# A graph network's first LayerNorm scaled on ScalarE, with a power, a leaky step and a maximum placed anew and the weights' preparation spread over the first iterations

## The chip, the cores and the metric

The kernel runs on one core of a Trainium2 chip. The metric is the device time of one execution in microseconds (us). Engines: PE is TensorE's matmuls, PEld its weight loads, DVE is VectorE, ACT is ScalarE, POOL is GpSimd. SBUF and PSUM are the two memories that the kernel's tiles are declared in; its matmuls write tiles of PSUM, in what the kernel calls banks. The granted clock is the share of TensorE's full clock that the profile's clock records show: 1.00 is full. The profiles are single executions; the times are medians.

## The reference, cut to what matters

Two layers over 128 graphs of 128 nodes with 512 features.

```python
# layer 0: graph attention (8 heads of 64), residual, LayerNorm "a"
feats = einsum('bnf,hfu->bhnu', X, W)
dense = leaky_relu(e_self[..., :, None] + e_neigh[..., None, :], 0.2)
dense = dense + NEG_BIG * (1.0 - A)
x = layernorm(x + relu(softmax(dense) @ feats + b))
# layer 1: two hypergraph convolutions, the first with relu and a LayerNorm behind it; residual; LayerNorm "o"
h = layer_norm(relu(hypergraph_conv(x, adj, W1, b1)), gamma, beta)
x = layernorm(x + hypergraph_conv(h, adj, W2, b2) + x)
```

## The kernel before

64 pairs of graphs go through a software pipeline. Iteration t runs stage 0 of pair t, stage 1 of pair t-1, and so on to stage 4. Each step has a lag and a time within the iteration (a period is some 43 us), and the steps' order by that time is the order of every engine's instructions.

The parts that matter: the mask is added on POOL, the leaky step is on ACT, the maximum on DVE.

```python
    for (g, q), tm, (lag, tl), (lagx, tx), te in (
        ((0, 0), 33.0, (1, 34.9), (1, 37.3), 9.5), ((0, 1), 34.3, (1, 36.2), (1, 38.3), 10.8),
        ((1, 0), 35.6, (1, 40.6), (2, 3.5), 12.6), ((1, 1), 36.9, (2, 2.9), (2, 4.3), 13.9),
    ):
        at(1, tm, masked, g, q)          # POOL, 128x512
        at(lag, tl, leaky, g, q)         # ACT, four of 128x128
        at(lagx, tx, largest, g, q)      # DVE
```

The first LayerNorm ("a"): statistics on DVE, the power on POOL as the end of the second graph's statistics, the scaling on DVE.

```python
    def moments(p, s, key, t, g):
        ... # bn_stats, bn_aggr
        if g == 1:  # the lines that allocate the tiles are cut
            nc.vector.tensor_scalar(ve, s["mv", key][:, :, 1], EPS, None, op0=ALU.add)
            nc.gpsimd.tensor_tensor(s["rs", key], ve, mhalf, op=ALU.pow)

    def normalize(s, key, t, g):
        nc.vector.tensor_scalar(t, t, s["mv", key][:, g, 0:1], s["rs", key][:, g:g + 1],
                                op0=ALU.subtract, op1=ALU.mult)

    at(2, 31.3, residual, 0)
    at(2, 33.2, residual, 1)
    @step(2, 35.7)
    def first_output(p, s):
        for g in range(2):
            normalize(s, "a", s["y"][:, g, :], g)
```

The matrix products are done as seven smaller ones in a chain. Products 1, 6, 7 and 4 use the PSUM bank X; ACT copies it out three times on the way. In the chain `py`, product 4 (time 39.2) must wait, by the program, until the third copy (time 38.0) has read the bank.

```python
    chain("py", 3, (29.2, 30.95, 32.7, 34.4, 36.2, 39.2, 40.9, 31.0, 34.5, 38.0), weigh,
          QU, 1)
    # seven products in the order 1, 2, 6, 5, 7, 4, 3, then ACT's three copies of bank X
```

The preparation of the weights stands in blocks: `prepare_first()` ahead of the loop, `prepare_hidden()` and `prepare_output()` at the end of iteration 1, `prepare_output_blocks()` (16 scalings and four block sums of 128x1024, all on DVE) ahead of iteration 2. `nodes` (time 10.4, DVE) makes the two scaled adjacency matrices of a pair.

## Time and profile before

| | before |
|---|---|
| time, median of 3 (range) | 2877.6 us (2877.2 to 2879.2) |
| profiled execution, span | 2872.6 us |
| mean granted TensorE clock | 0.990 |
| PE's waits for ACT's third copy of py | 69.3 us, 62 times |
| first pz matmul (layer 1 of the first pair) | 106.76 us |

Two of these numbers divide the run: up to the first pz matmul the pipeline fills, and PE idles a good part of the time; from there on PE is the bound, and its only recurring idle time is the wait for that copy. The lines themselves are in the prediction.

### The profile page before, as it was taken

To read this page: it belongs to the slowest core of one execution; us is meant where nothing else is said; L and a number is where in the kernel's file an instruction comes from. 1 tells how busy PE (TensorE), PEld (TensorE's weight loads), DVE (VectorE), ACT (ScalarE), POOL (GpSimd) and SP (SyncE) were. 2 spreads that over 40 slices of the span, in tenths; PEclk is the share of its full clock that TensorE was granted. 3 is DMA by queue.
4 is the path that set the end of the run, shared out by engine and by line. 5 is a ranking of instruction groups with operands and counts; after the bars stand their busy time and mean duration, and the time that the engine had idled before them with its cause. 6 is when DMAs were issued, how large, how long until landed. Compare 5 with 4: busy or idle time off the path is not lost.

```text
span 2872.6 us, 50435 instructions
## 1 busy us (share of the span) xinstructions
PE 2718.0 (95%) x18272; PEld 2476.4 (86%) x18272; DVE 1904.6 (66%) x4335; ACT 1590.2 (55%) x4549; POOL 1714.7 (60%) x1806
## 2 busy tenths in 40 slices
PE   3799999999999999999999999999999999999997
PEld 2688888888988888988988988988988988988986
DVE  4566666676676676676676676676676676676664
ACT  1465565565565555555555655655655655655652
POOL 3356656656656656656656656656656566566554
PEclk8799999999999999999999999999999999999999
DMA  4111111112112112112112112111112112112110
GB/s 143 45 48 61 60 47 62 59 44 65 58 44 67 46 55 67 46 56 67 45 56 67 42 60 67 43 59 67 42 60 67 42 60 67 42 60 67 41 38 23
DMA packets 99660, 161.61 MB, mean 56 GB/s; under 512 B 11602, under 2 KB 48466, under 8 KB 99412
## 3 DMA queue, kind: packets, MB, share of 16 engines
q1 hardware_dynamic: 95424, 156.80, 17.2%
q8 instruction: 146, 2.39, 0.3%
q10 hardware_dynamic: 3988, 1.59, 0.3%
q14 instruction: 102, 0.84, 0.1%
HBM read 124.27 MB, written 34.08 MB: 55 GB/s over the span
## 4 chain that ended last, share of the span: by engine, by line
PE 61%; POOL 21%; DVE 9%; ACT 6%; issue 3%; DMA 1%; POOLq 0%; SPq 0%; DVEq 0%; ACTq 0%
PE phX L615 16%; POOL hS L369 8%; PE phW L615 8%; PE pyX L387 8%; POOL sq L666 8%; PE pyW L387 5%; DVE y L533 5%; PE pz L579 4%; PE phY L615 4%; PE pfX L387 4%; PE pq L736 4%; DVE statsa L541 2%; PE pav L502 2%; ACT nb L449 2%; POOL nb L442 2%
## 5 line engine op out<-in xcount | busy, mean ns | idle before, releaser
L449 ACT ACTIVATE nb<-nb,ft 128x128 f32<-128x128 f32 x1024 | 327.0, 391 | 171.1 <-POOL nb L442 161.0
L442 POOL TENSOR_TENSOR nb<-nb,neg 128x512 f32<-128x512 f32 x256 | 343.1, 1361 | 101.1 <-DMA nb<-rd 101.1
L615 PEld LDWEIGHTS phX<-zS,w_sb 128*128 128x128 f32 x3072 | 363.0, 192 | 31.3 <-issue 31.3
L615 PE MATMUL phX<-zS,w_sb 128*128 128x128 f32 x3072 | 374.2, 275 | 0.8 <-ACT ph L254 0.8
L254 ACT COPY py<-pyX 128x257 f32<-128x257 f32 (+1 forms) x192 | 70.4, 366 | 490.7 <-PE pyX L387 490.7
L666 POOL TENSOR_TENSOR sq<-sq 128x512 f32<-128x512 f32 (+2 forms) x384 | 311.1, 817 | 20.1
L387 PE MATMUL pyX<-w_sb,h 128*128 128x257 f32 (+1 forms) x1024 | 253.1, 389 | 69.5 <-ACT py L254 69.3
L462 ACT ACTIVATE nb<-nb,nm 128x128 f32<-128x128 f32 x1024 | 312.9, 391 | 0.0
L645 ACT ACTIVATE h<-h,b_sb 128x128 f32<-128x128 f32 x768 | 244.5, 390 | 116.1 <-DVE h L630 116.1
L547 POOL TENSOR_TENSOR rso<-veo,mhalf 128x2 f32<-128x2 f32 x64 | 44.9, 701 | 421.0 <-DVE veo L545 421.0
L369 POOL TENSOR_TENSOR hS<-h 128x512 f32<-128x512 f32 x128 | 160.1, 1272 | 180.0 <-ACT h L645 180.0
L387 PEld LDWEIGHTS pyX<-w_sb,h 128*128 128x128 f32 x1024 | 184.2, 190 | 95.9 <-ACT py L254 74.9
L387 PE MATMUL pyX<-w_sb,hS 128*128 128x257 f32 (+1 forms) x1024 | 244.3, 381 | 2.5 <-POOL hS L369 2.5
L533 DVE SCALAR_TENSOR_TENSOR y<-y,x 128x512 f32<-128x512 f32 x128 | 184.5, 1441 | 91.6 <-POOL y L526 91.6
L387 PE MATMUL pyW<-w_sb,hS 128*128 128x256 f32 x1024 | 242.4, 378 | 2.1 <-DVE y L698 2.1
L502 PE MATMUL pav<-ft,eT 128*128 128x65 f32 x2048 | 239.5, 272 | 1.9 <-ACT eT L489 1.9
L502 PEld LDWEIGHTS pav<-ft,eT 128*128 128x128 f32 x2048 | 237.4, 192 | 2.1 <-ACT eT L489 2.1
L387 PEld LDWEIGHTS pyX<-w_sb,hS 128*128 128x128 f32 x1024 | 194.7, 190 | 31.5 <-POOL hS L369 2.9
L387 PEld LDWEIGHTS pyW<-w_sb,hS 128*128 128x128 f32 x1024 | 193.6, 189 | 30.4 <-DVE y L698 2.5
L550 DVE TENSOR_SCALAR y<-y,mva,rsa 128x512 f32<-128x512 f32 x128 | 183.2, 1470 | 52.2 <-POOL rsa L547 52.2
L603 POOL TENSOR_TENSOR zS<-zT 128x256 f32<-128x256 f32 x128 | 93.4, 730 | 205.3 <-ACT zT L590 205.3
L410 DVE TENSOR_TENSOR ft<-pf,pfW 128x264 f32<-128x264 f32 x128 | 55.1, 430 | 237.9 <-ACT pf L254 167.5
(128 smaller groups left out, 6167.9 us busy)
## 6 DMA issues: line engine op xcount, KB each, us to landing
nb<-rd SPq DMA_DIRECT2D x128, 512.0 KB, 4.5
x<-in_x_dram SPq DMA_DIRECT2D x64, 512.0 KB, 5.9
out_dram<-o SPq DMA_DIRECT2D x64, 512.0 KB, 2.8
a<-in_adj_dram SPq DMA_DIRECT2D x64, 128.0 KB, 5.0
w<-in_adj_dram SPq DMA_DIRECT2D x128, 64.0 KB, 4.8
w_sb<-in_w1t_dram SPq DMA_DIRECT2D x3, 512.0 KB, 6.5
w_sb<-in_w2t_dram SPq DMA_DIRECT2D x3, 512.0 KB, 9.6
w_raw<-in_w_dram SPq DMA_DIRECT2D x4, 256.0 KB, 4.7
```

The source lines that it names most:

```text
L369: engine.tensor_tensor(t[:, i], in0, in1, op=op)
L387: nc.tensor.matmul(to[:, :n], lhs[:, k, :], rhs[:, k, :n], start=bool(start) and k == 0, stop=(k == nk - 1), skip_group_check=True,)
L442: nc.gpsimd.tensor_tensor(t, t, s["neg"][:, g, None, :].to_broadcast([P, HH, N]), op=ALU.add)
L449: nc.scalar.activation(t, t, AF.Prelu, bias=s["ft"][:, g, h, 0:1], alpha=SLOPE)
L462: nc.scalar.activation(t, t, AF.Exp, bias=s["nm"][:, g, h:h + 1])
L502: nc.tensor.matmul(t[:, h * (U + 1):(h + 1) * (U + 1)], s["eT"][:, g, q * HH + h, :], s["ft"][:, g, q * HH + h, 2:], start=True, stop=True,)
L533: nc.vector.scalar_tensor_tensor(y, y, 0.0, s["x"][:, g, :], op0=ALU.max, op1=ALU.add)
L550: nc.vector.tensor_scalar(t, t, s["mv", key][:, g, 0:1], s["rs", key][:, g:g + 1], op0=ALU.subtract, op1=ALU.mult,)
L579: nc.tensor.matmul(t[:, k * N:(k + 1) * N], s["y"][:, g, k * P:(k + 1) * P], s["R"][:, g, :], start=True, stop=True,)
L615: nc.tensor.matmul(to[:, m * N:(m + 1) * N], w[:, k, m * P:(m + 1) * P], rhs[:, k, :], start=bool(start) and m == 0 and k == 0, stop=(k == ...
L645: nc.scalar.activation(dst[:, k, :], src[:, k, :], AF.Relu, bias=b1_sb[:, c:c + 1])
L666: nc.gpsimd.tensor_tensor(t[:, :n, :], t[:, :n, :], t[:, n:2 * n, :], op=ALU.add)
```

## The change

Its intent has two parts. In the steady state, the leaky step of the second mask leaves ACT's queue ahead of the third copy of `py`, so that PE's wait gets shorter; the scaling of LayerNorm "a" moves from DVE to ACT, as `Identity(rs * y + sh)` with a small new DVE instruction for `sh = -mean * rs`. At the start, the weights' preparation is cut into pieces among the first iterations, so that PE gets work earlier.

```diff
-    ... ((0, 1), 34.3, (1, 36.2), (1, 38.3), 10.8),
+    ... ((0, 1), 34.3, (1, 39.8), (1, 40.9), 10.8),
         # the power leaves moments() and becomes a step behind the second mask (34.3)
+    at(2, 35.5, rstds, "a")
-    @step(2, 35.7)
-    def first_output(p, s):
-        for g in range(2):
-            normalize(s, "a", s["y"][:, g, :], g)
+    @step(2, 36.3)
+    def first_shift(p, s):
+        s["sh"] = small.tile([P, 2], F32, tag="sh", name=f"sh_{p}")
+        nc.vector.scalar_tensor_tensor(
+            s["sh"], s["mv", "a"][:, :, 0], -1.0, s["rs", "a"], op0=ALU.mult, op1=ALU.mult)
+    def first_output(p, s, g):
+        t = s["y"][:, g, :]
+        nc.scalar.activation(
+            t, t, AF.Identity, bias=s["sh"][:, g:g + 1], scale=s["rs", "a"][:, g:g + 1])
+    at(2, 36.6, first_output, 0)
+    at(2, 37.2, first_output, 1)
-    at(3, 38.5, y_sum, 1, 1, 2, "W")
+    at(3, 38.4, y_sum, 1, 1, 2, "W")
+    at(4, 15.7, rstds, "o")
         # preparation: load of the first x later; block sums and memsets on POOL instead of DVE
-        second_sums(nc.vector, [w2_sb[:, i, :, :QU] for i in range(7)], w2_12)
+        second_sums(nc.gpsimd, [w2_sb[:, i, :, :QU] for i in range(7)], w2_12)
+    once = {
+        0: [(11.0, prepare_first)],
+        1: [(27.7, prepare_hidden), (27.5, prepare_output), (28.0, prepare_output_sums)],
+        2: [(9.0, prepare_output_blocks), (9.5, prepare_output_block_sums)],
+    }
+        # in iteration 2, stage 1's steps before time 30 stand 17 earlier
```

More of the change, by code (lines that the diff above doesn't have):

```diff
@@ L94, in load, with load_x @@
             nc.sync.dma_start(s["w"][:, g, :], adj[2 * p + g, 0, :].partition_broadcast(P))
+        if p:
+            load_x(p)
+    def load_x(p):
+        s = st[p]
         s["x"] = work.tile([P, 2, F], F32, tag="x", name=f"x_{p}", bufs=3)
-        nc.sync.dma_start(s["x"], x[gs].rearrange("g n f -> n g f"))
+        nc.sync.dma_start(s["x"], x[2 * p:2 * p + 2].rearrange("g n f -> n g f"))
     load(0)
@@ L124 @@
     an_bc = spread(a_neigh, F, "an_bc")
+    load_x(0)
     b0_bc = spread(b0, F, "b0_bc")
@@ L187, in prepare_hidden @@
         nc.vector.tensor_tensor(s4, a12, s2, op=ALU.subtract)
+    gbs = const.tile([P, KH, 2], F32, name="gbs")
+    made = {}
     def prepare_output():
-        gbs = const.tile([P, KH, 2], F32, name="gbs")
         nc.vector.tensor_scalar(gbs[:, :, 0], gb[:, 0, :], 1.0 / DH, None, op0=ALU.mult)
         nc.vector.tensor_copy(gbs[:, :, 1], gb[:, 1, :])
-        pv = [bank(f"pv{j}") for j in range(2)]
+        pv = made["pv"] = [bank(f"pv{j}") for j in range(2)]
         for blk, i, j in w2_blocks:
@@ L201, in prepare_output, with prepare_output_sums @@
                 )
+    def prepare_output_sums():
+        pv = made["pv"]
         sums = const.tile([2, F], F32, name="sums")
@@ L209, in prepare_output, with prepare_output_blocks @@
             nc.scalar.dma_start(t, sums_d[c].partition_broadcast(P))
-        return gw
-    def prepare_output_blocks(gw):
+        made["gw"] = gw
+    def prepare_output_blocks():
+        gw = made["gw"]
         for blk, i, j in w2_blocks:
@@ L219, in prepare_output_blocks, with prepare_output_block_sums @@
                 )
-        second_sums(nc.vector, [w2_sb[:, i, :, :QU] for i in range(7)], w2_12)
+    def prepare_output_block_sums():
+        second_sums(nc.gpsimd, [w2_sb[:, i, :, :QU] for i in range(7)], w2_12)
         for i in (0, 1, 5):
-            nc.vector.memset(w2_sb[:, i, :, QU:], 1.0 / DH)
+            nc.gpsimd.memset(w2_sb[:, i, :, QU:], 1.0 / DH)
     steps = []
@@ L464 @@
     for (g, q), tm, (lag, tl), (lagx, tx), te in (
-        ((0, 0), 33.0, (1, 34.9), (1, 37.3), 9.5), ((0, 1), 34.3, (1, 36.2), (1, 38.3), 10.8),
+        ((0, 0), 33.0, (1, 34.9), (1, 37.3), 9.5), ((0, 1), 34.3, (1, 39.8), (1, 40.9), 10.8),
         ((1, 0), 35.6, (1, 40.6), (2, 3.5), 12.6), ((1, 1), 36.9, (2, 2.9), (2, 4.3), 13.9),
@@ L542, in moments, with rstds @@
         nc.vector.bn_aggr(s["mv", key][:, g, :], stats)
-        if g == 1:
-            ve = small.tile([P, 2], F32, tag="ve", name=f"ve{key}_{p}")
-            nc.vector.tensor_scalar(ve, s["mv", key][:, :, 1], EPS, None, op0=ALU.add)
-            s["rs", key] = small.tile([P, 2], F32, tag="rs", name=f"rs{key}_{p}")
-            nc.gpsimd.tensor_tensor(s["rs", key], ve, mhalf, op=ALU.pow)
+    def rstds(p, s, key):
+        ve = small.tile([P, 2], F32, tag="ve", name=f"ve{key}_{p}")
+        nc.vector.tensor_scalar(ve, s["mv", key][:, :, 1], EPS, None, op0=ALU.add)
+        s["rs", key] = small.tile([P, 2], F32, tag="rs", name=f"rs{key}_{p}")
+        nc.gpsimd.tensor_tensor(s["rs", key], ve, mhalf, op=ALU.pow)
     def normalize(s, key, t, g):
@@ L556 @@
     at(2, 33.2, residual, 1)
-    @step(2, 35.7)
-    def first_output(p, s):
-        for g in range(2):
-            normalize(s, "a", s["y"][:, g, :], g)
+    at(2, 35.5, rstds, "a")
[3 more added lines that the diff above has]
+        nc.vector.scalar_tensor_tensor(
+            s["sh"], s["mv", "a"][:, :, 0], -1.0, s["rs", "a"], op0=ALU.mult, op1=ALU.mult
+        )
+    def first_output(p, s, g):
+        t = s["y"][:, g, :]
+        nc.scalar.activation(
+            t, t, AF.Identity, bias=s["sh"][:, g:g + 1], scale=s["rs", "a"][:, g:g + 1]
+        )
+    at(2, 36.6, first_output, 0)
+    at(2, 37.2, first_output, 1)
     def skip(p, s, g):
@@ L764 @@
     last = max(lag for _, _, lag, _ in steps)
+    once = {
[3 more added lines that the diff above has]
+    }
     with tc.manual_schedule():
-        prepare_first()
         for t in range(PAIRS + last):
@@ L769 @@
                 load(t)
-            if t == 2:
-                prepare_output_blocks(gw)
-            for _, _, lag, fn in steps:
+            todo = [(time, fn, ()) for time, fn in once.get(t, ())]
+            for time, _, lag, fn in steps:
                 if 0 <= t - lag < PAIRS:
-                    fn(t - lag, st[t - lag])
-            if t == 1:
-                prepare_hidden()
-                gw = prepare_output()
+                    early = 17.0 if t == 2 and lag == 1 and time < 30.0 else 0.0
+                    todo.append((time - early, fn, (t - lag, st[t - lag])))
+            for _, fn, args in sorted(todo, key=lambda e: e[0]):
+                fn(*args)
             st.pop(t - last, None)
```

## The prediction

> **What bounds the kernel now.** First the page's shares: TensorE (PE) is busy 95% of the span, the other engines 55 to 66%, and PE's row is low only in the first slices.
>
> ```profile
> PE 2718.0 (95%) x18272; PEld 2476.4 (86%) x18272; DVE 1904.6 (66%) x4335; ACT 1590.2 (55%) x4549; POOL 1714.7 (60%) x1806
> PE   3799999999999999999999999999999999999997
> ```
>
> So I asked second what PE waited for: the waits of PE alone (total, times, longest).
>
> ```profile
> PE pyX L387 <- ACT py L254: 69.3, 62, 1.8
> PE pfX L387 <- ACT pf L254: 21.4, 2, 20.9
> PE pv L198 <- issue: 16.6, 1, 16.6
> PE pa L306 <- DVE hD L280: 12.3, 1, 12.3
> PE pt L295 <- DMA x<-in_x_dram: 10.3, 1, 10.3
> PE pz L579 <- ACT nb L449: 7.2, 1, 7.2
> ```
>
> One wait recurs: once per pair, 69.3 us over 62, 1.12 us each. In the steady state the list of PE's gaps holds nothing else, so a period of some 43.2 us is 42.1 us of matrix work and this gap. The other lines are start-up: up to the first pz matmul at 106.76 us PE idles 68 us.
>
> Third, the timeline around one such gap (start, length):
>
> ```profile
> 1222.99 1.27 POOL L442 TENSOR_TENSOR nb<-nb,neg 128x512 f32<-128x512 f32 x1 [1.50 <-DMA nb<-rd]
> 1223.23 1.58 DVE L533 SCALAR_TENSOR_TENSOR y<-y,x 128x512 f32<-128x512 f32 x1
> 1225.79 0.17 DVE L545 TENSOR_SCALAR vea<-mva 128x2 f32<-128x2 f32 x1
> 1226.04 0.70 POOL L547 TENSOR_TENSOR rsa<-vea,mhalf 128x2 f32<-128x2 f32 x1 [1.77 <-DVE vea L545]
> 1226.71 4.09 POOL L442 TENSOR_TENSOR nb<-nb,neg 128x512 f32<-128x512 f32 x3
> 1226.78 2.89 DVE L550 TENSOR_SCALAR y<-y,mva,rsa 128x512 f32<-128x512 f32 x2 [0.81 <-POOL rsa L547]
> 1228.02 1.28 ACT L449 ACTIVATE nb<-nb,ft 128x128 f32<-128x128 f32 x4 [2.44 <-POOL nb L442]
> 1229.20 0.35 ACT L254 COPY py<-pyX 128x256 f32<-128x256 f32 x1
> 1229.60 2.00 PE L387 MATMUL pyX<-w_sb,h 128*128 128x256 f32 x8 [1.50 <-ACT py L254]
> ```
>
> The reader sees a chain: variance (vea), power (rsa, 0.70), second mask (1.27), its leaky step (1.28), and only then the copy of py, which had stood behind the leaky step in ScalarE's queue. From the power's end to PE's start is 2.77 us on average (the power ends 1.66 us before PE runs dry, PE starts 1.11 after).
>
> Fourth, the start-up:
>
> ```profile
> 53.06 3.57 PE L198 MATMUL pv<-w_sb,gbs 128*2 128x256 f32 x8 [16.58 <-issue]
> 70.30 3.25 DVE L216 SCALAR_TENSOR_TENSOR w_sb<-w_sb,gb,gw 128x256 f32<-128x256 f32 x8
> 85.38 2.10 PE L387 MATMUL pfX<-w_sb,xS 128*128 128x264 f32 x4 [20.94 <-ACT pf L254]
> 106.76 3.76 PE L579 MATMUL pz<-R,y 128*128 128x128 f32 x16 [7.19 <-ACT nb L449]
> ```
>
> The preparation stands as one block: VectorE is at it, or waits for it, from 46.1 to 78.2 us, and the second pair's features wait until 85.
>
> [...]
>
> ```profile
> 1235.81 0.73 POOL L603 TENSOR_TENSOR zS<-zT 128x256 f32<-128x256 f32 x1 [3.24 <-ACT zT L590]
> 1236.13 0.43 DVE L331 TENSOR_SCALAR deg<-deg 128x2 f32<-128x2 f32 x1
> ```
>
> A 128x2 instruction takes 0.17 free and 0.43 here; it ends 0.02 after GpSimd's. In 61 of 61 cases it was so. Likewise the two normalizations in the fence above: 0.54 each free, 1.48 each beside masks, the first ending 0.28 after the mask.
> [...]
>
> **The change part by part.**
> 1. Steady state. Leaky step and maximum of the second mask go behind the copy of py: its 1.28 leaves the path. The power goes behind the second mask: that 1.27 leaves the path too where the mask is done by the time vea is ready. But the two normalizations leave VectorE (2 x 1.45 measured, beside PE's path) and come to ScalarE as two ACTIVATEs *ahead of* the copy of py, after a new 128x2 instruction on VectorE (first_shift, two SBUF inputs).
>  - vea: VectorE's second residual (L533) waits for the first mask and ends 0.55 after it. The second mask now follows at once, but waits in turn: it would end about 1.68 after the first (xS beside skip shows such a delay of 0.4). vea is ready then, 1.70, as today. The power ends at the same moment as before.
>  - The third mask starts 0.03 before the power's end, first_shift 0.04 after it, as the normalization does today (126 of 126 waited). So first_shift ends at 1.24 + 0.02 = 1.26 after the power instead of 0.2.
>  - ScalarE: 0.03 to start; [...] copy 0.35, overlapping by 0.09; 0.05 to PE. Sum: 1.26 + 0.03 + 1.54 - 0.09 + 0.35 + 0.05 = 3.14, against 2.77: the gap grows by 0.37.
>  - In 7 of 62 gaps the first mask came so late (DMA) that the residual went ahead of it. There the power now waits for the second mask too, some 1.1 more.
>  Worked through gap by gap with the measured mask ends, 69.3 us become 94.7: **+25 us**.
>  Behind the copy nothing new binds: x evictions 1.06, leaky 1.28, y copy 0.37 and leaky 1.28 end 3.98 after it, before the first pz eviction at 4.66.
> 2. Start-up (each time an estimate from durations in the trace). VectorE's nodes go ahead of the first weights, whose loads go ahead of x; but the second pair's nodes still wait for adj rows that landed at 28.7 behind the large weights, say 27.8 now. Rows go out at some 31.9 instead of 35.6. pv (9 us) starts then instead of at 53, sums land and ScalarE's queue, which waits for them, is free at 43.7. The second pair's features end at 54 (ahead of the first pair's softmax), VectorE scales 16 blocks (6.4) until 60.6, nodes and eT copies until 64, attention until 66. GpSimd now makes the block sums: 4 x 2.35 (1.27 at 512 columns, 0.73 at 256, so 2.35 at 1024) from 60.6 to 70.3, and add_bias stands behind: 72.8; residuals, statistics, power, shift, scaling 7.1: first pz at about 80 instead of 106.8. **-27 us**, give or take 6. Hidden is what PE itself does; the gain is idle time alone.
> 3. y_sum 0.1 earlier, last power 0.1 later: nothing waits for them. Tail: no masks, so none of the above; 0 to -2.
>
> Sum: 2877.6 + 25 - 27 = 2876.
>
> **The rivals.**
> (a) *first_shift isn't blocked* (too small, or let in before the third mask). Then it ends 0.2 after the power, the path is 2.0 to 2.1 instead of 3.14, the gaps shrink to 24 us: -45, with start-up 2877.6 - 45 - 27 = 2806, faster by 2.5%. For it: the author put it there, and a [128,2] scalar_tensor_tensor beside a mask occurs nowhere in this trace. Against it: 61 of 61 blocked 128x2 instructions[...]. I give it one in eight.
> (b) *The second mask doesn't wait for the residual, the residual for it*: residual and power end 0.7 to 1.1 later in all 62 gaps, about +50 us, 2925. Against it: beside skip and in the normalizations the two engines alternate, GpSimd never got two in a row over a waiting VectorE.
> (c) *Start-up hidden or worse*: GpSimd's block sums hold up add_bias; if they ran 4 us each, or pv stayed slow at the 0.57 clock of 40 to 60 us, only 15 to 20 us remain: 2885. If ScalarE isn't held by sums, 5 us more are gained.
>
> **Range and chances.** Three quarters of the weight lie at 2866 to 2892, an eighth at 2800 to 2815, the rest between (shift blocked in part only, a larger start-up gain). So 2872, range 2810 to 2892. 2% faster is 2820, reached by (a) only with most of the start-up gain: 0.13. 2% slower is 2935: 0.02. Same 0.85.
>
> **What would show it.** PE pyX behind ACT py: total near 95 us in the waits (24 for (a)). The new shift line: mean near 1.2 us (0.16 for (a)), released by or beside the third mask; the ACTIVATE of y 0.8. First pz at 75 to 86. The period 43.6 instead of 43.2. Wrong if the shift is short, if PE's gap moved elsewhere (phX behind zT, say), or if first pz is still near 100.

In the sum of step 1 the 1.54 for the two ACTIVATEs is the author's estimate. The trace before shows 0.630 us for a 128x512 ACTIVATE without scale and bias columns (L655, 256 of them); what the columns add it does not show.

## The result, and the profile after

The changed kernel takes **2903.8 us** (median of 4, 2899.6 to 2909.2) where the kernel before takes 2877.4 in the same rounds. Ratios are computed as the mean time of one kernel's fast runs over that of the other's of the same rounds, so they are not quite the ratio of the medians; here it is 1.0091, with a 95% interval of 1.0074 to 1.0109. So it is 0.9% slower. "Same" at the 2% mark was right; 2872 and the range up to 2892 were not.

The shares of the page after, the same two lines as of before:

```profile
PE 2746.9 (95%) x18272; PEld 2496.4 (86%) x18272; DVE 1814.8 (63%) x4264; ACT 1678.1 (58%) x4677; POOL 1725.3 (59%) x1813
PE   5899999999999999999999999999999999999997
```

The first slices have filled, as hoped. But PE is busy 28.9 us *longer* than before with the same 18272 instructions. That is the first sign of what was missed.

The waits of PE after (total, times, longest):

```profile
PE pyX L401 <- ACT py L268: 96.6, 63, 3.0
PE pt L309 <- DMA x<-in_x_dram: 13.9, 1, 13.9
PE pav L516 <- DVE eT L503: 9.8, 1, 9.8
PE pz L607 <- ACT y L584: 6.5, 1, 6.5
```

The recurring wait grew from 69.3 to 96.6 us. The two waits of start-up of 16 to 21 us are gone, and one of 9.8 is new.

The timeline around one wait after (start, length, and in brackets the idle time ahead and what ended it):

```profile
962.63 0.70 POOL L563 TENSOR_TENSOR rsa<-vea,mhalf 128x2 f32<-128x2 f32 x1
963.30 2.49 POOL L456 TENSOR_TENSOR nb<-nb,neg 128x512 f32<-128x512 f32 x2
963.37 1.22 DVE L578 SCALAR_TENSOR_TENSOR sh<-mva,rsa 128x2 f32<-128x2 f32 x1 [0.81 <-POOL rsa L563]
964.62 1.52 ACT L584 ACTIVATE y<-y,sh,rsa 128x512 f32<-128x512 f32 x2 [2.46 <-DVE sh L578]
966.04 0.35 ACT L268 COPY py<-pyX 128x256 f32<-128x256 f32 x1
966.44 3.60 PE L401 MATMUL pyX<-w_sb,h 128*128 128x256 f32 x8 [1.81 <-ACT py L268]
```

The chain is the predicted one: power, third mask, the shift held for the length of that mask, two ACTIVATEs, copy, PE. The last line is not: the eight matmuls of product 4 take 3.60 us, where in the fence of before they took 2.00.

The shift and the scaling over the whole run, from the view of the shift's tile (minimum/median/maximum in ns, then first and last start):

```profile
L584 ACT ACTIVATE y<-y,sh,rsa x128: 797/806/815, 85.7 to 2851.2; 128x512 f32<-128x512 f32 x128
L578 DVE SCALAR_TENSOR_TENSOR sh<-mva,rsa x64: 161/1219/1228, 84.5 to 2850.3; 128x2 f32<-128x2 f32 x64
```

Why those matmuls are slow shows in the windows around the same wait (length, then busy us and instructions of PE, PEld, DVE, ACT, POOL, then PE's granted clock, DMA share and GB/s):

```profile
962.90:966.32 3.42, 1.73 (x15) 1.54 (x13) 1.81 (x2) 1.70 (x4) 3.27 (x4) 1.00 0.37 140
966.32:969.73 3.41, 3.29 (x8) 2.67 (x9) 1.57 (x6) 2.21 (x7) 0.70 (x1) 0.50 0.00 0
969.73:973.14 3.41, 3.41 (x24) 3.17 (x23) 1.33 (x3) 1.98 (x6) 0.00 (x0) 1.00 0.00 0
```

In the window that holds the wait PE is busy for 1.73 us, half of it. In the next 3.41 us the clock is 0.50, and then 1.00 again. The trace's clock records show 11 such stretches of 3.413 us between 130 and 2700 us, and a twelfth at 2809.5; the kernel before has none between 130 us and its last 70 us. The last 70 us, in which the pipeline drains, are counted apart here and below, as half clock shows there in the kernel before too (3.4 us at 2849.1, and from 2869.6 to the end at 2872.6). PE has work through nearly all of such a stretch (3.29 of 3.41 us in the one shown), so each is reckoned to cost half of it, 1.71 us.

### Where the time went

From the recorded matmuls each span is divided at the first pz matmul of the first pair and of the last pair:

| us | first pz at | PE busy from there to the last pair's pz | PE idle in that part | tail | span |
|---|---|---|---|---|---|
| before | 106.8 | 2646.5 | 74.1 | 45.3 | 2872.6 |
| after | 86.6 | 2670.1 | 99.2 | 45.3 | 2901.2 |
| difference | -20.2 | +23.6 | +25.1 | 0.0 | +28.6 (rounded parts: +28.5) |

The busy time, summed by tile in that part (each matmul from the end of the one ahead of it), grew at two tiles: pyX from 457.4 to 474.4 and pyW from 218.3 to 222.8 us, together 21.5. No other tile moved by more than 1.4. All but 1.8 of it is product 4 and product 3 behind it, the matmuls right behind the wait. The 1.8, and the 1.4 of pav, come from one more stretch, of 6.83 us, in the drain (2836.8 to 2843.7), where the kernel before has none; PE is busy throughout, so it costs 3.4. The 12 stretches at 1.71 us are 20.5, with this one 23.9, against 23.6 measured. So the half clock explains the longer busy time.

The start-up after, in the timeline:

```profile
59.67 5.32 POOL L170 TENSOR_TENSOR w_sb<-staged,w_sb 128x1024 f32<-128x1024 f32 x1 [10.34 <-DVE staged L228]
63.00 2.13 DVE L284 SCALAR_TENSOR_TENSOR junk<-a,w 128x128 f32<-128x128 f32 x1
65.18 2.25 DVE L289 TENSOR_SCALAR dn<-dd 128x2 f32<-128x2 f32 x1
69.60 2.52 DVE L294 TENSOR_SCALAR hD<-a,dn 128x128 f32<-128x128 f32 x2
72.97 5.38 PE L516 MATMUL pav<-ft,eT 128*128 128x65 f32 x24 [9.84 <-DVE eT L503]
86.60 3.78 PE L607 MATMUL pz<-R,y 128*128 128x128 f32 x16 [6.54 <-ACT y L584]
```

POOL's block sums run beside DVE's `nodes` of the third pair, and hold them four times for about 2 us (three of the four are shown). Nodes last from 62.7 to 72.1 us, so the copies of the attention weights start at 72.3 and PE's attention at 73.0.

### The profile page after: what moved, and what is told of

It is laid out like the page before. It is cut to its first block, busy times and chain, and to the rows that moved or that the text cites. A ratio compares the mean times of both kernels' runs of the same rounds, so it can differ in the third digit from the quotient of the medians.

```text
span 2901.2 us, 50436 instructions
## 1 busy us (share of the span) xinstructions
PE 2746.9 (95%) x18272; PEld 2496.4 (86%) x18272; DVE 1814.8 (63%) x4264; ACT 1678.1 (58%) x4677; POOL 1725.3 (59%) x1813
## 4 chain that ended last, share of the span: by engine, by line
PE 52%; POOL 23%; DVE 13%; ACT 5%; issue 4%; DMA 2%; POOLq 0%; SPq 0%; ACTq 0%; DVEq 0%
PE phX L643 16%; POOL hS L383 10%; POOL sq L694 9%; PE phW L643 8%; PE pyX L401 6%; DVE y L547 5%; PE pyW L401 4%; PE pz L607 4%; PE phY L643 4%; PE pq L764 4%; PE pfX L401 3%; DVE statsa L555 3%; DVE sh L578 3%; POOL y L540 2%; ACT h L673 2%
## 5 line engine op out<-in xcount | busy, mean ns | idle before, releaser
L456 POOL TENSOR_TENSOR nb<-nb,neg 128x512 f32<-128x512 f32 x256 | 345.5, 1371 | 99.2 <-DMA nb<-rd 97.1
L401 PE MATMUL pyX<-w_sb,h 128*128 128x257 f32 (+1 forms) x1024 | 270.1, 409 | 96.7 <-ACT py L268 96.6
L401 PEld LDWEIGHTS pyX<-w_sb,h 128*128 128x128 f32 x1024 | 194.2, 200 | 126.6 <-ACT py L268 102.1
L469 DVE TENSOR_REDUCE nm<-nb 128x4 f32<-128x512 f32 x256 | 174.4, 682 | 103.1 <-ACT nb L463 103.1
L401 PEld LDWEIGHTS pyX<-w_sb,hS 128*128 128x128 f32 x1024 | 194.7, 190 | 31.6 <-POOL hS L383 2.9
```

What stands on the lines that cost most here:

```text
L401: nc.tensor.matmul(to[:, :n], lhs[:, k, :], rhs[:, k, :n], start=bool(start) and k == 0, stop=(k == nk - 1), skip_group_check=True,)
L456: nc.gpsimd.tensor_tensor(t, t, s["neg"][:, g, None, :].to_broadcast([P, HH, N]), op=ALU.add)
L469: nc.vector.tensor_reduce(s["nm"][:, g, hs], s["nb"][:, g, hs, :], AX.X, ALU.max, negate=True)
```

## The experiments

The theory after reading the traces: three terms, start-up (-20), longer waits (+25 of idle time; +27 in the one recurring wait), half clock after some waits (+21). Rivals: the slow matmuls are slowed by something else that comes with the ACTIVATEs, not by the idle time ahead; or start-up and steady state act on each other. Each line of results gives the median, and the ratio to the kernel before in the same rounds with its 95% interval.

### 1. The two halves of the change apart

`startup_only` is the changed kernel with the steady state of before; `steady_only` is the kernel before with the steady state of the change.

```diff
 # startup_only, against the changed kernel
-    at(2, 35.5, rstds, "a") ... first_shift, first_output on ACT
+    @step(2, 35.7) first_output with normalize on DVE; power back in moments()
-    ((0, 1), 34.3, (1, 39.8), (1, 40.9), 10.8)
+    ((0, 1), 34.3, (1, 36.2), (1, 38.3), 10.8)
 # steady_only, against the kernel before: the same lines the other way round
```

> The changed kernel with the steady state of before put back (normalization on VectorE, power and leaky step at their old places); only the preparation in pieces is left. Theory A (the change is three terms: start-up -20, longer wait before the fourth py product +27, half clock after some of these waits +20): 2877 - 20 = 2857 us, first pz near 86 us, waits of PE behind the copy of py near 69 us, no half-clock stretch between 130 and 2780 us. Rival B (the pieces disturb the first iterations and cost time later): over 2870 us.

> The kernel before with only the steady-state part of the change (scaling on ScalarE, power, leaky step and maximum moved). Theory A: 2877 + 27 + 20 = 2924 us, waits behind the copy of py near 96 us, some 12 half-clock stretches of 3.4 us between 130 and 2780 us, give or take 6. Rival B (the loss sits in the new start-up): near 2877 us.

`startup_only`: 2853.1 us, 0.9924 (0.9908 to 0.9939), -22 us. First pz at 88.2, the wait 66.0 us, no half-clock stretch between 130 us and the last 70. `steady_only`: 2923.1, 1.0167 (1.0152 to 1.0182), +48 us. First pz at 109.4, the wait 94.9, 11 stretches up to 2700 us and a twelfth at 2829.8; pyX and pyW 21.4 us longer than before.

The halves add up: -22 and +48 make +26, and the whole change measured +26. They do not act on each other in any size that matters. And the steady half alone has the half clock: it doesn't come from the start-up.

### 2. PE kept busy in the wait

If idle time is what halves the clock, matmuls that nobody reads, put in the wait, should take the stretches away although nothing else changes. First with eight (`gap_filled`), then with four (`gap_half_filled`).

```diff
+    @step(3, 39.1)
+    def fill(p, s):
+        for _ in range(8):      # gap_half_filled: 4
+            nc.tensor.matmul(s["pm"][:, 128:256], ident, ident, start=True, stop=True)
```

> The changed kernel with eight matmuls added whose result nobody reads, placed where PE waits for the copy of py (0.9 us a pair, 57 us of PE work in all). Theory A (PE's clock is halved for one 3.41 us window after a window in which PE was idle for over some 45%): the waits shrink to about 96 - 57 = 40 us, no window is idle that long, the half-clock stretches in the steady state vanish, and the time falls by about 20 us to 2884 in spite of more work. Rival C (the half clock comes of load, heat or chance, not of the gap's length): the stretches stay and the time stays at 2904, or rises.

> As the filled gap, with four matmuls instead of eight: the eight took 1.8 us a pair (two passes each), so that they were longer than the wait and added work of their own; four take 0.9 us and fit inside nearly every wait (least 1.03 us). Theory A (half clock follows an idle stretch, not load): the end of the wait is unmoved, no window is idle for over 45%, no half-clock stretches in the steady state, 2904 - 20 = 2884 us. Rival C: 2904 us, stretches as in the changed kernel.

`gap_filled`: 2896.9, 1.0076 (1.0061 to 1.0091). No half-clock stretch was left ahead of the drain, but the gain was nearly nil: the profile lists two matmuls for each of these (x16 for the eight), which took 2.0 us instead of the 0.9 that I had reckoned with, ran over the end of the wait (3.1 us left of it) and delayed product 4. The run speaks for the theory by its clock and says nothing by its time; the fill was the wrong size.

`gap_half_filled`: 2880.1, 1.0014 (0.9999 to 1.0029). No stretch ahead of the drain either, and the time is 22 us below the changed kernel's, by the two ratios to the kernel before (1.0091 and 1.0014 of 2877). In its timeline:

```profile
1214.40 1.14 PE L744 MATMUL pm<-ident 128*128 128x128 f32 x8
1215.04 1.52 ACT L584 ACTIVATE y<-y,sh,rsa 128x512 f32<-128x512 f32 x2 [1.87 <-DVE sh L578]
1216.46 0.35 ACT L268 COPY py<-pyX 128x256 f32<-128x256 f32 x1
1216.86 2.00 PE L401 MATMUL pyX<-w_sb,h 128*128 128x256 f32 x8 [1.33 <-ACT py L268]
```

The scaling on ACT and the copy are as before; PE restarts no sooner; only its idle time is split, and product 4 takes 2.00 us. Useless work made the kernel 0.8% faster. That rules out the rival: the ACTIVATEs are still there.

The control is the kernel before with the same four matmuls (`before_half_filled`):

> A control: the kernel before with the same four unread matmuls in its waits (which are 0.6 to 1.8 us there, so the 0.9 us overhang 13 or so of them by up to 0.3). Theory A: before has no half-clock stretch in its steady state to lose, so nothing is gained: 2875 us, or up to 5 us more. Rival C2 (unread matmuls help in some other way, by keeping PE's queue or clock better in general): 20 us less, 2855.

2874.9, 1.0003 (0.9982 to 1.0025): no change. Its wait fell from 69.3 to 10.1 us, filled with useless work, and its trace has no half clock ahead of the drain to be rid of. So these four matmuls a pair were worth 22 us where the clock had halved, and nothing where it had not.

### 3. The shift not held up

The shift as two instructions of one column each, with one tensor and a column as the scalar, in the place of one instruction with two tensors (`shift_one_column`).

```diff
-        nc.vector.scalar_tensor_tensor(
-            s["sh"], s["mv", "a"][:, :, 0], -1.0, s["rs", "a"], op0=ALU.mult, op1=ALU.mult)
+        for g in range(2):
+            nc.vector.tensor_scalar(
+                s["sh"][:, g:g + 1], s["mv", "a"][:, g, 0:1], s["rs", "a"][:, g:g + 1], -1.0,
+                op0=ALU.mult, op1=ALU.mult)
```

> The changed kernel with the shift made by two tensor_scalar instructions of 128x1 instead of one scalar_tensor_tensor of 128x2 with two SBUF tensors. Theory A (the shift waits 1.2 us for the third mask[...]): two instructions of 0.17 us, the wait of PE falls by about 0.85 us a pair, from 96 to about 45 us, no half clock; 2904 - 51 - 20 = 2833 us. Rival D (the shift's length is the power's result coming late, or any VectorE instruction waits): the first of the two takes 1.2 us as before, and the time is 2904 or slightly more.

2819.0, 0.9800 (0.9784 to 0.9816). From the view of the shift's tile:

```profile
L579 DVE TENSOR_SCALAR sh<-mva,rsa x128: 202/210/216, 85.0 to 2768.0; 128x1 f32<-128x1 f32 x128
```

Not one of 128 was held. The wait fell to 31.6 us, where 45 was expected, and so the time is below the expected 2833. The reason is that the first scaling needs the first column alone: in one period of this trace it starts 0.25 us after the shift (2041.60 and 2041.85), against 1.25 in the fence of the changed kernel. Of the stretches one was left up to 2700 us and one at 2727.5. So the held shift, 1.22 us against 0.33 for the two together, was worth 65.0 us of wait (96.6 less 31.6) and ten half-clock stretches (ten times 1.71, 17 us): together 82, and the profiled spans differ by 82.1 (2901.2 and 2819.1). This is what the prediction's rival (a) would have been.

### 4. Order instead of speed

The leaky step is out of the way of the copy in the changed kernel; the scaling need not stand there either. `scale_behind_copy` puts the two ACTIVATEs behind the copy, whose time is 38.0. `leaky_alone` takes only the move of the leaky step (with the maximum that reads it) and leaves the scaling on DVE, with the start-up of the change.

```diff
 # scale_behind_copy, against the changed kernel
-    at(2, 36.6, first_output, 0)
-    at(2, 37.2, first_output, 1)
+    at(2, 38.2, first_output, 0)
+    at(2, 38.3, first_output, 1)
 # leaky_alone, against startup_only
-    ((0, 1), 34.3, (1, 36.2), (1, 38.3), 10.8)
+    ((0, 1), 34.3, (1, 39.8), (1, 40.9), 10.8)
```

> The changed kernel with the two scalings placed behind the copy of py in ScalarE's queue; the shift stays blocked by the third mask. Theory A (the loss is only that the copy stands behind shift and scaling): the waits of PE behind the copy go from 96 to under 10 us and the half clock goes with them: 2904 - 97 - 20 = 2787 us; the scalings then push x evictions, leaky step and pz evictions back by 1.5 us, which could cost up to 0.5 us a pair: 2787 to 2818. Rival E (PE is bound elsewhere as soon as this wait is gone): a new wait of about 1 us a pair and over 2840 us.

> The changed kernel with the normalization put back on VectorE and the power ahead of the second mask, as before: only the leaky step and the maximum of the second mask stand behind the copy of py, with the new start-up. Theory A: the copy waits for nothing but PE, yet VectorE is at the normalizations until 1.2 us after PE runs dry, so that the second sum of py comes late by about 0.35 us a pair: 2904 - 97 - 20 + 22 = 2809 us. Rival F (the move to ScalarE is what the change needs, VectorE becomes the bound without it): over 2850 us.

`scale_behind_copy`: 2779.5, **0.9666** (0.9651 to 0.9680). The wait for the copy is 0.2 us in all, and no stretch is left ahead of the drain:

```profile
PE pyW L401 <- DVE y L726: 0.4, 1, 0.4
PE pyX L401 <- ACT py L268: 0.2, 1, 0.2
```

The shift is still held, with a median of 1221 ns: off PE's path it costs nothing. The time is below the range that was expected (2787 to 2818). PE's restarts, which the expectation had left out, went with the waits: pyX is 8 us shorter than before, as product 4 begins 0.14 us before the matmuls ahead of it end, where after a wait nothing overlaps. Its own length hardly differs (1.98 us in 61 of 64 cases, against 2.00 after a wait).

`leaky_alone`: 2813.3, 0.9788 (0.9772 to 0.9805). The copy's wait is 0.2 as well, but a new one stands in its place, in its waits of PE:

```profile
PE pyW L401 <- DVE y L711: 19.9, 52, 0.8
```

By the program a DVE sum must read bank W before product 3 may add to that bank. In one period of the trace DVE is at the two scalings beside the masks from 1228.19 to 1231.09 us, then makes a maximum, and starts this sum at 1231.61, although the copy that it needs was done at 1229.30. PE's loss is larger than the wait: pyW's busy time is 233.6 us against 218.3 before. So moving the scaling to ACT does have a use, but only together with the right place: it frees DVE for that sum. In `scale_behind_copy` this wait is 0.4 us in all, once (the first line of its fence above).

### 5. The start-up

In the changed kernel `nodes` (10.4) stands behind the blocks (9.0 and 9.5). `shift_nodes_first` moves them behind `nodes`, on top of `shift_one_column`.

```diff
-        2: [(9.0, prepare_output_blocks), (9.5, prepare_output_block_sums)],
+        2: [(10.5, prepare_output_blocks), (10.55, prepare_output_block_sums)],
```

> The kernel with the one-column shift, and the third pair's nodes ahead of the output blocks' preparation. In the changed kernel the nodes ran 62.7 to 72.0 us beside GpSimd's block sums and took 9.3 us instead of 1.9 (blocked four times), and the eT copies stood behind them. Theory A: nodes near 56 to 58 us in 1.9 us, eT copies 7 us earlier, the first pz about 4 us earlier (add_bias still waits for the block sums): 2819 - 4 = 2815 us. Rival: first pz unmoved at 86 us, as the block sums alone set it.

2814.6, 0.9788 (0.9774 to 0.9803). In its start-up:

```profile
59.30 0.48 DVE L294 TENSOR_SCALAR hD<-a,dn 128x128 f32<-128x128 f32 x2
66.96 5.38 PE L516 MATMUL pav<-ft,eT 128*128 128x65 f32 x24 [1.27 <-DVE eT L503]
```

Against `shift_one_column`, nodes last 1.7 us (58.04 to 59.8) instead of 9.4, PE's wait for the attention weights is 1.3 instead of 9.8, and attention starts 6.5 us earlier (66.96 for 73.47). First pz is at 82.9 instead of 86.1: only 3.2 us are left of those 6.5, because the bias on POOL now waits for the block sums, as the prediction had it. The time itself can't confirm so small a gain: the two kernels ran on different chips, and the intervals of their ratios overlap. The trace shows it.

### 6. Both together

`best` is `scale_behind_copy` with nodes ahead of the blocks (the two diffs above).

> The scalings behind the copy of py and the nodes ahead of the blocks' preparation, both alterations together. Theory A: they lie in different stretches and add: 2779 - 4 = 2775 us, first pz near 81 us, no half clock from 130 us to the tail.

2775.5, **0.9654** (0.9630 to 0.9678), 3.5% faster than before and the fastest of all; first pz at 81.0. Its timeline at the place where the wait was:

```profile
1213.69 0.37 ACT L268 COPY py<-pyX 128x256 f32<-128x256 f32 x1 [0.52 <-PE pyX L401]
1213.77 1.22 DVE L578 SCALAR_TENSOR_TENSOR sh<-mva,rsa 128x2 f32<-128x2 f32 x1 [1.90 <-POOL rsa L563]
1214.67 1.98 PE L401 MATMUL pyX<-w_sb,h 128*128 128x256 f32 x8
1215.03 1.52 ACT L584 ACTIVATE y<-y,sh,rsa 128x512 f32<-128x512 f32 x2 [0.97 <-DVE sh L578]
```

The copy follows the bank's last matmul by half a microsecond, product 4 has no wait before it, and shift and scaling are beside it. Whether it is faster than `scale_behind_copy` by more than chance is not shown: their intervals overlap, and they ran on different chips.

## Why the prediction was wrong, point by point

- **The wait (step 1): total and mechanism right, one term misread.** Predicted 94.7 us in all, measured 96.6. Its terms: shift 1.26 after the power, with the median of the held instruction at 1.219 us; each ACTIVATE 0.82 and a pair 1.54, estimates that the trace before did not show, measured 0.806 and 1.52; product 4 restarting after the copy. The sum of 3.14 was measured as 3.10. But the 2.77 from the power's end to PE's start that it was set against is misread: the prediction's own fence gives 2.86 (1226.74 to 1229.60), and all 62 gaps have 2.85 to 2.86. So the path grew by 0.24, not 0.37. The rest of the 0.4 us came from the power, which ended later against PE's work (PE ran dry 1.56 us after it instead of 1.74, on average); the prediction had that in seven gaps alone. That the total fits within 2 us is in this part luck. Rival (a) is false as the kernel stands (and true of the one-column form, experiment 3); rival (b) is false.
- **The start-up (step 2): mechanism right, size off.** Predicted -27 (give or take 6), measured -20.2 in the trace and -22 in experiment 1. The term is "nodes and eT copies until 64": they ended at 73.5 instead (the copies last 1.27 us from 72.25), because nodes took 9.4 us beside POOL's block sums. The prediction reckoned with DVE being held beside POOL for the shift and not for nodes. Of the sums themselves the first took 5.32 us instead of 2.35. It began beside eight scalings on DVE (59.51 to 62.76 us) and ended 2.23 us after the last of them. Rival (c) had the size, 15 to 20 us, but for another reason: the other three sums took 2.2 to 2.3 us, not 4. Some of the loss was hidden, as the sums hold the bias up anyway: experiment 5 got 3.2 us of it back.
- **The step that failed: "a period of some 43.2 us is 42.1 us of matrix work and this gap".** It took the matrix work as a constant to which the wait is added. It isn't one. When the wait got 0.4 us longer on average, PE was idle for about half of a 3.41-us window in some iterations, and ran the next window at half clock. This added 20.5 us which no term of the sum had, and the stretch in the drain 3.4 more. With these 24 us and the 7 missing from the start-up (27 less 20) the sum of 2876 becomes 2907, against 2903.8 measured, and 2906 by the two profiled executions (2877.6 and their difference of 28.6). Experiment 2 shows the cause of the 12 stretches (the idle time taken away and all else left), and the traces of its control and of the kernel before have none of them.
- **Why only 12 of 63.** The stretches begin on a grid of 3.413 us, so it matters where on that grid a wait lies. From the recorded matmuls of the changed kernel: each of the 11 stretches up to 2700 us follows a window of the grid in which PE was busy for 37 to 54% of the time, and of the windows without such a consequence four had 52 to 54% and all others 56% or more. In `steady_only` the stretches follow 36 to 53%, the others have 49% and more. The least busy window of the kernel before has 55%: it stood right above the edge, with waits only 0.4 us shorter. The longest wait of the changed kernel, 2.98 us up to 2107.9 us, brought no stretch: the grid has an edge at 2106.4, in the middle of it, so neither window lost more than half.
- **What stays open.** The edge isn't sharp: windows with the same share went either way (52% at 785.4 us with a stretch behind it, 52% at 519.2 us without), and `startup_only` has one of 49% without a stretch. Nor does the busy share decide alone: in the drain of the changed kernel a window of 63% (2833.4 to 2836.8 us, with the attention's matmuls of 65 columns in it) was followed by the 6.83 us of half clock, and in `scale_behind_copy` one of 75%. Why is not settled. Whether some matmuls count less than others isn't settled; with the transposes (pt, pet, pa, pr) left out of the share, the cases separated worse: in the changed kernel the windows ahead of the 11 stretches then have 30 to 44%, and 13 others lie between 32 and 43%. How far the number of stretches varies from run to run is open too, since only one run of each kernel has a trace. The spread of the times doesn't tell: four runs of the changed kernel lie within 9.6 us and four of `steady_only`, with as many stretches in its trace, within 1.0. The kernel before may have a few at times: of its seven runs beside `best` one took 2880.3 us at a granted clock of 0.986, where five with 0.989 took 2868.2 to 2873.6.

The range was too narrow for the same reason: all its uncertainty was in the wait and the start-up, none in the speed of PE behind the wait.

## What to carry to other kernels

When an engine's wait grows, check the speed of what comes after it, and not only its length: compare the busy time of the same instructions in both traces, tile by tile, and the granted clock in windows around the wait. Moving work to a less busy engine puts it in that engine's queue: here two ACTIVATEs (1.52 us a pair) *ahead of* the copy that frees bank X lay in PE's wait of 96.6 us in all; the same two behind that copy left 0.2 us of it and made this kernel 3.3% faster than before instead of 0.9% slower. Where POOL is given work beside DVE, go through every DVE instruction next to it (four of `nodes` took 1.9 to 2.4 us here in place of 0.16 to 0.29), not only the one that the change adds.

## What the traces showed of the clock, of DVE beside POOL, and of ACT

- The clock: the stretches at 1.00 and 0.50 begin and end on a grid of 3.413 us in both traces. In the changed kernel, which lost some 20 us in this way, half clock came after windows in which PE was busy for up to 54% (1.73 of 3.42 us in the one shown), behind waits of 1.55 to 2.22 us, while a wait of 2.98 us that lay across the grid at 2106 us was followed by none. In the steady state of these runs the share of the window counts, with an edge near 50 to 55%; in the drain that did not hold (half clock after 63%). The prediction has no term for it.
- DVE beside POOL: a 128x2 scalar_tensor_tensor took 1219 ns beside a mask against 161 free. Of tensor_scalar, a 128x2 one was held in the start-up (2.25 us at 65.18 us, 0.17 free), and the one-column form of experiment 3 never was (202 to 216 ns in 128 cases, at the same place beside the masks); a reciprocal of 128x2 beside a block sum wasn't either (0.17 us at 67.47 us). What tells them apart these runs do not show. When both engines had more to do, they alternated in the start-up: four DVE instructions beside the four sums each ended 0.02 to 0.19 us after a sum, and lost 1.7 to 2.2 us each.
- ACT: 128x512 with scale and bias as columns took 0.806 us (797 to 815 ns in 128 cases), without them 0.630 in the trace before.
